# Folding layer 3's router weights: queries first, on quarters of TensorE's columns

## The chip, the cores and the metric

The kernel runs on one core of a Trainium2 chip. The metric is the device time of one execution in microseconds (us), given as the median of several runs. A core has five engines with a queue of instructions each: TensorE (PE in the profile; its loads of weights are PEld) multiplies matrices into the accumulation memory, PSUM; VectorE (DVE), ScalarE (ACT) and GpSimd (POOL) work element by element; SyncE (SP) issues most of the DMA transfers. The engines run side by side and wait for each other through semaphores.

## The reference

The input has 8 blocks of 128 tokens with 512 numbers each. Four layers follow one another, each a "conditioned" part and a feed-forward part whose result is added to x. Only layer 3's last part matters here. Its conditioned part gives y = base(x) + 2 * (low-rank experts), and its feed-forward part picks 16 of 64 experts by the scores

```python
q = jnp.einsum('bsd,rd->bsr', x, Wq_w)          # Wq_w: 16 x 512
scores = jnp.einsum('bsr,er->bse', q, keys)     # keys: 64 x 16
top_vals, top_idx = jax.lax.top_k(scores, TOP_K)
```

where this x is y, so `base = jnp.einsum('btd,od->bto', x, W)` (W: 512 x 512) and the experts' output matrix B (512 x 128 in all) come before it. Scores are linear in y, so the kernel never forms y: it folds keys, Wq and W into one matrix of 512 x 64 (the "fk" product), which is applied to x, and keys, Wq and B into one of 128 x 64 (the "gk" product), which is applied to the gated middle of the experts. Products of three matrices can be taken in two orders: (keys Wq) first, then times W; or (Wq W) first, then times keys.

## The kernel before

The program is one `forward` of some 2300 lines. A tile framework orders each engine's instructions and sets the semaphores. After layers 0 and 1 comes layer 2's attention, a hand-ordered loop of 32 steps, then the `ending`, which holds layer 2's feed-forward part and layer 3.

`open3` allocates layer 3's tiles in a pool (`w3`) and loads them by SyncE, one transfer after the other: Bm in four transfers, `base` (1 MB), `wq` (each of the four chunks of 128 rows has 16 columns), `keysT` (16 partitions by 64), `wB`, `wmr` (the middle's and the router's weights, with 64 columns left free for the folded scores), and `BwT` (1 MB). SyncE's queue is in order, so a transfer that waits holds up those behind it. The load of the attention's sums for their check (`all`, line 750) follows.

`layer2` multiplies the eight blocks of tokens by layer 2's matrix: `product`, tile `h`, 16 matmuls of 128x128 for each block (line 1753 is the helper's). The matmuls leave their sums in PSUM banks, where `delta` adds the low-rank part for four blocks at a time; then VectorE adds the bank to x (line 1929), which frees it. Between the products, layer 3's weights are prepared by two generators, stepped once a block: `weights_turned` transposes base, wB and wq by TensorE, and `fold_scores` makes the folded score matrices. Their banks have the tag "st" once delta(0) is through, three buffers, which were those of h for blocks 0, 1 and 2. ScalarE copies each result to memory (`copied`, line 1955).

Layer 2's routing runs beside: VectorE, with exponentials on ScalarE at lines 1874 and 1885 (tiles p and m), ends in p, which TensorE transposes (`pT`, line 1901) and turns into `pmix`; VectorE then makes `zp` (line 1910), which delta(0) reads.

`fold_scores` in the kernel before takes keys times the transposed queries (kwp, four matmuls whose contraction has 16 rows), then for each of four chunks of columns four accumulating matmuls with W (fkp, 16 matmuls with 64 columns moved), then four with wBT (gkp).

`layer3` follows: `mids` (midp, tile wmr read), `route` on VectorE, `fold_ranks` (fp, with sums W3s made by GpSimd at line 2003), `mix`, `fold_last` (gp), `scores` (sc), `ranks` (z), `turned` (zT) and `last` (o), which writes the output. GpSimd also makes the sums Bws from BwT[...].

A matmul of 32-bit numbers leaves two records in the profile. If its weights have 32 columns, and its result lies in one of four groups of 32 partitions, it takes a quarter of TensorE's columns. The helper `slot(j)` names such a group, and `mmq` is the matmul without a check of groups; `low` (tile z, 128 columns moved) and the down-projection's low rank (tile td, 256 columns moved, line 362) use quarters already.

Of the kernel before, what the change touches and what calls it, by code (L numbers as in the profile page):

```python
# [10 lines left out]
F32 = mybir.dt.float32  # L11
# [6 lines left out]
P = 128  # L18
NB = 8
NT = NB * P  # L20
D = 512
DC = D // P
# [1710 lines left out]
def ending(  # L1733
    tc, a, out, x, ident, bias3, experts, early, tile_of_w2, tile_of_aw, room, chunks, mm, kept=lambda i: i
# [5 lines left out]
    pe, act, dve, pool, sp = nc.tensor, nc.scalar, nc.vector, nc.gpsimd, nc.sync  # L1740
    NE, NR = 64, 8
# [7 lines left out]
    def slot(j):  # L1749
        return slice(j * 32, (j + 1) * 32)  # L1750

    def mmq(o, lhsT, rhs, start, stop):
        return pe.matmul(o, lhsT, rhs, start=start, stop=stop, skip_group_check=True)  # L1753
# [7 lines left out]
    L3 = SimpleNamespace()  # L1761
# [37 lines left out]
    def turn(y2, b, bank):  # L1799
        if not Y2T:  # L1800
            Y2T.append(early.tile([P, DC, NT], F32, tag="yT", name="y2T"))
        ps = bank("mm", [P, DC, P], f"y2T_{b}")
        for c in range(DC):
            pe.transpose(ps[:, c, :], y2[:, b, c * P : (c + 1) * P], ident)
        (act.copy if b % 2 else dve.tensor_copy)(Y2T[0][:, :, b * P : (b + 1) * P], ps)

    def low(g, bank):

        ps = bank("mm", [P, P], f"z2_{g}")
        for c in range(DC):  # L1810
            for j in range(HB):
                b = g * HB + j
                mmq(ps[slot(j), :], A2[:, c, :], Y2T[0][:, c, b * P : (b + 1) * P], c == 0, c == DC - 1)
        dve.tensor_copy(zq[:, g, :], ps)

    def anchors(g, bank):
        ps = bank("mm", [P, 2, 16], f"hd_{g}")
        for i in range(2):
            t0 = (2 * g + i) * 2 * P
            for c in range(DC):  # L1820
                mm(ps[:, i, :], Y2T[0][:, c, t0 + 1 : t0 + 2 * P : 2], WH[:, c, :], c == 0, c == DC - 1)
        dve.tensor_tensor(
            hd[:, 2 * g : 2 * g + 2, :], ps, b16.unsqueeze(1).to_broadcast([P, 2, 16]), ALU.add
        )
# [8 lines left out]
    def product(b, tag, bank):  # L1833

        ps = bank(tag, [P, DC, P], f"h_{b}")
        for o in range(DC):
            for c in range(DC):
                mmq(
                    ps[:, o, :], W["2"][:, c, o * P : (o + 1) * P], Y2T[0][:, c, b * P : (b + 1) * P],
                    o == 0 and c == 0, False,  # L1840
                )
        H[b] = ps
# [53 lines left out]
    def gains(bank):  # L1896

        p = Z["p"]
        pt = bank("mm", [P, NA, P], "pT2")
        for i in range(NA):  # L1900
            pe.transpose(pt[:8, i, :], p[:, i, :], ident)
        pT = L3.w3.tile([8, NA * P], F32, tag="pT", name="pTs2")
        act.copy(pT, pt[:8].rearrange("p i t -> p (i t)"))
        pm = bank("mm", [P, TG, 64], "pmix")
        for g in range(TG):
            for j in range(HB):
                b = g * HB + j
                mmq(pm[slot(j), g, :], Li, pT[:, b * 64 : (b + 1) * 64], g == 0, True)
        zp = L3.w3.tile([P, TG, P], F32, tag="zp", name="zp")
        dve.scalar_tensor_tensor(  # L1910
            zp.rearrange("p g (t two) -> p g t two", two=2),
            zq.rearrange("p g (t two) -> p g t two", two=2),
            0.5,
            pm.unsqueeze(3).to_broadcast([P, TG, 64, 2]),
            ALU.mult,
            ALU.mult,
        )
        Z["zp"] = zp

    def delta(g):  # L1920

        zp, Bm = Z["zp"], L3.Bm
        for o in range(DC):
            for j in range(HB):
                mmq(H[g * HB + j][:, o, :], Bm[slot(j), o * P : (o + 1) * P], zp[slot(j), g, :], False, True)
        for j in range(HB):
            b = g * HB + j
            t = x[:, :, b * P : (b + 1) * P]
            dve.tensor_tensor(t, H[b], t, ALU.add)
# [3 lines left out]
    def open3(w3, ex_sm):  # L1933
        def load(name, shape, src):
            t = w3.tile(shape, F32, tag=name, name=name)
            sp.dma_start(t, src)
            return t

        L3.w3 = w3
        L3.Bm = w3.tile([P, D], F32, tag="Bm", name="Bm2")  # L1940
        for j in range(4):
            sp.dma_start(L3.Bm[slot(j), :], a["Bmat"])
        L3.base = load("base3", [P, DC, D], chunks(a["base3"]))
        L3.wq = load("Wq3", [P, DC, 16], chunks(a["Wq3"]))
        L3.keysT = load("keysT", [16, NE], a["keysT"])
        L3.wB = load("wB3", [P, D], a["wB3"])
        L3.wmr = w3.tile([P, DC, WR], F32, tag="wmr3", name="wmr3")
        sp.dma_start(L3.wmr[:, :, 0:136], chunks(a["wmr3"]))
        L3.Bw = load("BwT", [P, DC, D], chunks(a["BwT"]))
        L3.steps = experts("l3", L3.wmr, "logits", 2.0, bias3, None, None, x, None, width=WR)  # L1950
        L3.zgT = w3.tile([P, DC, NT], F32, tag="zgT", name="zgT")

    def copied(shape, name, ps, dst=None):
        t = L3.w3.tile(shape, F32, tag=name, name=name) if dst is None else dst
        act.copy(t, ps)
        return t

    def weights_turned(bank):

        L3.W = L3.w3.tile([P, DC, D], F32, tag="W3", name="W3")  # L1960
        for o in range(DC):
            ps = bank("mm", [P, DC, P], f"W3p_{o}")
            for d in range(DC):
                pe.transpose(ps[:, d, :], L3.base[:, d, o * P : (o + 1) * P], ident)
            copied(None, None, ps.rearrange("p c d -> p (c d)"), L3.W[:, o, :])
            yield
        ps = bank("mm", [P, DC, P], "wB3p")
        for o in range(DC):
            pe.transpose(ps[:, o, :], L3.wB[:, o * P : (o + 1) * P], ident)
        L3.wBT = copied([P, DC, P], "wB3T", ps)  # L1970
        yield
        ps = bank("mm", [P, D], "wq3p")
        for o in range(DC):
            pe.transpose(ps[:16, o * P : (o + 1) * P], L3.wq[:, o, :], ident)
        L3.wqT = copied([16, D], "wq3T", ps[:16])

    def fold_scores(bank):
        ps = bank("mm", [P, DC, NE], "kwp")
        for o in range(DC):
            mm(ps[:, o, :], L3.wqT[:, o * P : (o + 1) * P], L3.keysT, True, True)  # L1980
        kw = copied([P, DC, NE], "kw3", ps)
        yield
        ps = bank("mm", [P, DC, NE], "fkp")
        for d in range(DC):
            for o in range(DC):
                mm(ps[:, d, :], L3.W[:, o, d * P : (d + 1) * P], kw[:, o, :], o == 0, o == DC - 1)
        copied(None, None, ps, L3.wmr[:, :, 136:WR])
        yield
        ps = bank("mm", [P, NE], "gkp")
        for o in range(DC):  # L1990
            mm(ps, L3.wBT[:, o, :], kw[:, o, :], o == 0, o == DC - 1)
        L3.GK = copied([P, NE], "gk3", ps)


# [191 lines left out]
    def layer2(y2, bank, held=lambda: None, do=range(NB)):  # L2186

        for b in do:
            turn(y2, b, bank)
        for g in range(TG):  # L2190
            if g or len(do) > HB:
                low(g, bank)
                anchors(g, bank)

        where = ["mm"]

        def free(tag, shape, name):
            return bank(where[0], shape, name)

        turning, folding = weights_turned(free), fold_scores(free)  # L2200
        for b in range(HB):
            if b not in H:
                product(b, "av" if b == HB - 1 else "st", bank)
                next(turning)
        routing()
        gains(bank)
        product(HB, "av", bank)
        next(turning)
        delta(0)
        where[0] = "st"  # L2210
        for b in range(HB + 1, NB):
            product(b, "mm", bank)
            for _ in turning:
                pass
            next(folding, None)
        delta(1)

    def layer3(bank, between=lambda: None):
# [37 lines left out]
    return SimpleNamespace(  # L2256
        prepare=prepare, load_w2=load_w2, load_aw=load_aw, turn=turn, low=low, anchors=anchors,
        product=product, shifted=shifted, open3=open3, layer2=layer2, layer3=layer3,
    )

# [64 lines left out]
```

## Time and profile before

| | us |
|---|---|
| median of 3 runs | 1501.79 |
| lowest and highest run | 1498.33, 1505.07 |
| the profiled execution | 1500.54 |
| its span, first to last instruction | 1498.7 |
| TensorE busy | 1483.4 |
| VectorE busy | 1066.7 |
| GpSimd busy | 855.7 |
| ScalarE busy | 562.5 |
| granted TensorE clock, share of full speed | 0.997 |

All times in views of the trace are counted from the first instruction of the profiled execution. A line of the timeline has start, length, engine, line of code, operation, result and operands, shape and count; in brackets stands how long the engine was idle before, and what ended the idle time. The chain of waits is followed back from the last instruction: at each step to what released it, or to the instruction before it on its engine. The prefix "in_" marks an input in device memory; buffer numbers are left out of names.

### The profile page before, as it was taken

How to read it: one execution, taken by the hardware profiler on the slowest of the kernel's cores; microseconds unless marked ns; L12 is line 12 of the kernel's file. 1: busy time of each engine (PE TensorE's matmuls, PEld its weight loads, DVE VectorE, ACT ScalarE, POOL GpSimd, SP SyncE). 2: the span in 40 equal slices, each digit the busy share in tenths (PEclk: the TensorE clock that was granted, in tenths of full speed). 3: DMA queues.
4: the chain of work that ended last, by engine and by line, in shares of the span. 5: the costliest groups of instructions: out<-in, count | busy, mean ns of one | idle time of the engine just before them, and what ended most of it. 6: DMA issues, size and time to landing. Idle time of an engine off the chain costs nothing.

```text
span 1498.7 us, 18133 instructions
## 1 busy us (share of the span) xinstructions
PE 1483.4 (99%) x5629; PEld 943.6 (63%) x5629; DVE 1066.7 (71%) x2121; ACT 562.5 (38%) x1422; POOL 855.7 (57%) x874
## 2 busy tenths in 40 slices
PE   9999999999999999999999999999999999999998
PEld 7888787455555655555555555565555565559887
DVE  4566524388888787877778778787878878854475
ACT  1111101044444554454554444455444455431110
POOL 2232103567776777777777777677777777621210
PEclk9999999999999999999999999999999999999999
DMA  7311001313646444554454455345445534432001
GB/s 240 118 43 33 1 1 51 97 32 102 172 136 206 139 120 130 154 183 127 134 150 127 125 150 179 121 134 159 126 129 164 167 106 138 120 106 93 2 6 54
DMA packets 154985, 171.43 MB, mean 114 GB/s; under 512 B 52480, under 2 KB 125376, under 8 KB 154752
## 3 DMA queue, kind: packets, MB, share of 16 engines
q1 hardware_dynamic: 136736, 133.17, 30.2%
q0 software_dynamic: 17056, 36.49, 7.9%
q8 instruction: 47, 0.77, 0.2%
q10 hardware_dynamic: 1088, 0.52, 0.1%
q14 instruction: 58, 0.48, 0.1%
HBM read 129.35 MB, written 40.76 MB: 114 GB/s over the span
## 4 chain that ended last, share of the span: by engine, by line
PE 91%; DVE 4%; DMA 2%; POOL 1%; issue 1%; ACT 0%; SPq 0%; ACTq 0%; DVEq 0%; POOLq 0%
PE st L1165 17%; PE av L1217 17%; PE g L362 8%; PE q_six L971 8%; PE wo_two L971 6%; PE q_one L971 5%; PE q_five L971 5%; PE dn L362 5%; PE wo_six L971 4%; PE wo_one L971 4%; PE eo_l L53 3%; PE h L1753 2%; PE z L1753 2%; PE midp_l L53 1%; PE o L1753 1%
## 5 line engine op out<-in xcount | busy, mean ns | idle before, releaser
L914 POOL DMA_INDIRECT kn<-in_k_cache,kvrow_k x256 | 270.3, 1056 | 77.1 <-issue 70.9
L914 POOL DMA_INDIRECT vals<-in_v_cache,kvrow_v x256 | 271.6, 1061 | 73.5 <-issue 58.4
L1217 PE MATMUL av<-pT,vals 128*128 128x512 f32 x640 | 290.7, 592 | 0.2 <-DVE oT L1227 0.2
L1169 ACT ACTIVATE pT<-st,hide 128x512 f32<-128x512 f32 x256 | 176.0, 687 | 194.0 <-PE st L1165 173.1
L1165 PE MATMUL st<-qT,kT 128*128 128x512 f32 x512 | 237.7, 597 | 1.0 <-DMA qT<-turned_new 0.8
L1217 PEld LDWEIGHTS av<-pT,vals 128*128 128x128 f32 x640 | 121.4, 190 | 152.7 <-issue 149.0
L1070 POOL TENSOR_TENSOR vq<-q,txq 128x256 f32<-128x256 f32 x128 | 121.2, 978 | 135.1 <-ACT sqq L1044 95.6
L1165 PEld LDWEIGHTS st<-qT,kT 128*128 128x128 f32 x512 | 96.9, 191 | 111.7 <-issue 104.8
L1185 DVE TENSOR_TENSOR part<-pT 128x512 f32<-128x512 f32 x128 | 88.4, 692 | 76.9 <-ACT pT L1169 66.7
L971 PE MATMUL q_one<-q,x 128*128 128x384 f32 x256 | 93.0, 486 | 0.0
L1044 ACT ACTIVATE sqq<-q 128x128 f32<-128x128 f32 x252 | 78.2, 310 | 11.8 <-DVE q L1020 5.1
L971 PEld LDWEIGHTS q_one<-q,x 128*128 128x128 f32 x256 | 48.5, 190 | 39.8 <-issue 14.1
L971 PE MATMUL q_six<-q_s,xs_all 128*128 128x384 f32 x192 | 69.8, 486 | 0.0
L1025 ACT COPY q<-q_one 128x256 f32<-128x256 f32 x32 | 11.9, 372 | 150.4 <-PE q_one L971 133.5
L971 PE MATMUL wo_one<-o,oT 128*128 128x256 f32 x256 | 65.8, 379 | 0.2 <-DVE oT L1227 0.2
L1165 PE MATMUL st<-qT,kTn 128*128 128x512 f32 x128 | 65.4, 592 | 0.0
L971 PE MATMUL wo_two<-o_s,os 128*128 128x256 f32 x256 | 60.6, 380 | 1.8 <-DVE vals L1020 1.5
L429 POOL TENSOR_TENSOR ws<-wu 128x256 f32<-128x256 f32 (+1 forms) x9 | 6.4, 713 | 91.8 <-DMA wu<-in_WuT 81.0
L1169 ACT ACTIVATE pT<-st,rs 128x512 f32<-128x512 f32 x64 | 44.0, 687 | 38.5 <-PE av L1217 25.7
L971 PEld LDWEIGHTS wo_one<-o,oT 128*128 128x128 f32 x256 | 48.6, 190 | 13.8 <-issue 0.5
L1201 ACT COPY rows<-rows 32x32 f32<-32x32 f32 x96 | 20.7, 216 | 92.8 <-DVE rows L1196 64.2
L362 PE MATMUL g<-xs,ws 128*128 128x256 f32 (+1 forms) x240 | 55.2, 379 | 0.0
(459 smaller groups left out, 2853.0 us busy)
## 6 DMA issues: line engine op xcount, KB each, us to landing
turned_new<-qkt SPq DMA_DIRECT2D x120, 160.0 KB
turned_cached<-kt SPq DMA_DIRECT2D x128, 128.0 KB
kT<-turned_cached SPq DMA_DIRECT2D x32, 512.0 KB
R<-sums SPq DMA_DIRECT2D x32, 512.0 KB
qT<-turned_new SPq DMA_DIRECT2D x30, 512.0 KB
q<-in_WqT SPq DMA_DIRECT2D x8, 1024.0 KB
o<-in_WoT SPq DMA_DIRECT2D x8, 1024.0 KB
kn<-in_k_cache,kvrow_k POOLq DMA_INDIRECT x256
```

Of the source, the lines that this page charges most:

```text
L53: pe.matmul(o, lhsT, rhs, start=start, stop=stop)
L362: pe.matmul(o, lhsT, rhs, start=start, stop=stop, skip_group_check=True)
L914: kept(pool.indirect_dma_start(out=d[:, c, :], out_offset=None, in_=kc if what == "k" else vc, in_offset=bass.IndirectOffsetOnAxis(ap=kvro ...
L971: kept(pe.matmul(o, l[:, c, :], r[:, c, :], start=start and c == 0, stop=c == 1, skip_group_check=True))
L1044: kept(act.activation(sq, S[n][m][:, j, i, :], AF.Square, accum_out=S[n]["ssq"][:, j, col : col + 1]))
L1070: kept(pool.tensor_tensor(to, t[:, b, :, hi : hi + 64], wx[:, b, lo : lo + 64].unsqueeze(2).to_broadcast(list(to.shape)), ALU.mult,))
L1165: kept(pe.matmul(ps, s["kT"][:, c, 4 * j : 4 * j + 4, :] if c < 4 else s["kn"][:, j], s["qT"][:, :, REP * j : REP * (j + 1), :].rearrange( ...
L1169: kept(act.activation(pT[:, c, :, :].rearrange("p i t -> p (i t)"), ps, AF.Exp, **(dict(bias=hide[:, b, c : c + 1]) if c < 4 else dict(bia ...
L1185: kept(dve.tensor_tensor(o, l, r, ALU.add))
L1201: kept(act.copy(rows[0:32, g, :], rows[32 * g : 32 * g + 32, 0, :]))
L1217: kept(pe.matmul(ps, v[:, c, :], pT[:, c, :, :].rearrange("p i t -> p (i t)"), start=c == 0, stop=c == NC - 1, skip_group_check=True,))
L1753: return pe.matmul(o, lhsT, rhs, start=start, stop=stop, skip_group_check=True)
```

## The change

The query weights get a tile of 32 columns a chunk, of which 16 are loaded, and the keys a tile of 128 partitions: both are set to zero by GpSimd, and the keys are then loaded four times, to partitions 0, 32, 64 and 96. The transposition of wq falls away. `fold_scores` takes the queries first: for each chunk o of 128 rows it multiplies the queries' chunk by W's chunk in quarter o of the columns. The four quarters hold four partial sums on four groups of partitions. The product with the repeated keys then contracts over all 128 partitions and so adds the quarters; the rows between are zero. The same is done with wBT. `weights_turned` has one step less, so the calls of `next` are given a default.

```diff
         L3.base = load("base3", [P, DC, D], chunks(a["base3"]))
-        L3.wq = load("Wq3", [P, DC, 16], chunks(a["Wq3"]))
-        L3.keysT = load("keysT", [16, NE], a["keysT"])
+        L3.wq = w3.tile([P, DC, 32], F32, tag="Wq3", name="Wq3")
+        L3.keys = w3.tile([P, NE], F32, tag="keys4", name="keys4")
+        for t in (L3.wq, L3.keys):
+            pool.memset(t, 0.0)
+        sp.dma_start(L3.wq[:, :, 0:16], chunks(a["Wq3"]))
+        for j in range(4):
+            sp.dma_start(L3.keys[32 * j : 32 * j + 16, :], a["keysT"])
         L3.wB = load("wB3", [P, D], a["wB3"])
...
         L3.wBT = copied([P, DC, P], "wB3T", ps)
-        yield
-        ps = bank("mm", [P, D], "wq3p")
+
+    def fold_scores(bank):
+        ps = bank("mm", [P, D], "qwp")
         for o in range(DC):
-            pe.transpose(ps[:16, o * P : (o + 1) * P], L3.wq[:, o, :], ident)
-        L3.wqT = copied([16, D], "wq3T", ps[:16])
-
-    def fold_scores(bank):
-        ps = bank("mm", [P, DC, NE], "kwp")
+            mmq(ps[slot(o), :], L3.wq[:, o, :], L3.W[:, o, :], True, True)
+        qw = copied([P, D], "qw3", ps)
+        ps = bank("mm", [P, P], "qbp")
         for o in range(DC):
-            mm(ps[:, o, :], L3.wqT[:, o * P : (o + 1) * P], L3.keysT, True, True)
-        kw = copied([P, DC, NE], "kw3", ps)
+            mmq(ps[slot(o), :], L3.wq[:, o, :], L3.wBT[:, o, :], True, True)
+        qb = copied([P, P], "qb3", ps)
         yield
         ps = bank("mm", [P, DC, NE], "fkp")
         for d in range(DC):
-            for o in range(DC):
-                mm(ps[:, d, :], L3.W[:, o, d * P : (d + 1) * P], kw[:, o, :], o == 0, o == DC - 1)
+            mm(ps[:, d, :], qw[:, d * P : (d + 1) * P], L3.keys, True, True)
         copied(None, None, ps, L3.wmr[:, :, 136:WR])
-        yield
         ps = bank("mm", [P, NE], "gkp")
-        for o in range(DC):
-            mm(ps, L3.wBT[:, o, :], kw[:, o, :], o == 0, o == DC - 1)
+        mm(ps, qb, L3.keys, True, True)
         L3.GK = copied([P, NE], "gk3", ps)
...
-                next(turning)
+                next(turning, None)
         routing()
         gains(bank)
         product(HB, "av", bank)
-        next(turning)
+        next(turning, None)
```

## The prediction

> **What bounds the kernel now.** I read the busy line of the page first, then the chain of waits over the stretch that the change touches, then the timelines of ScalarE, VectorE, GpSimd and SyncE there, to see what stands beside the chain.
>
> ```profile
> PE 1483.4 (99%) x5629; PEld 943.6 (63%) x5629; DVE 1066.7 (71%) x2121; ACT 562.5 (38%) x1422; POOL 855.7 (57%) x874
> ```
>
> TensorE is busy for 99% of the span, so the question is whether its instructions in this stretch are themselves the chain. The chain of waits from 1374 to 1404 us (start, length, engine, tile, line, records; an fp32 matmul leaves two records, a transpose one):
>
> ```profile
> 1380.71 4.87 PE h L1753 x64
> 1385.58 0.44 PE wB3p L1969 x4
> 1386.02 0.44 PE wq3p L1974 x4
> 1386.45 0.89 PE h L1753 x8
> 1387.34 1.03 PE kwp L53 x8
> 1388.37 2.88 PE h L1753 x24
> 1391.25 3.52 PE fkp L53 x32
> 1394.77 3.63 PE h L1753 x32
> 1398.40 0.84 PE gkp L53 x8
> 1399.24 1.10 PE h L1753 x32
> ```
>
> Every piece is TensorE and each begins where the last ends: nothing is waited for. So each microsecond of TensorE taken out here is a microsecond of the chain, until another engine is late. Per record, fkp (64 columns moved) takes 3.52/32 = 0.110 us, no less than h (128 columns), 3.63/32 = 0.113. And h after kwp takes 2.88 for 24, where 24 x 0.112 = 2.69 would do: going back from a 16-row matmul to full ones costs 0.19.
>
> How fast are quarters of the columns? The chain at the down-projection shows the same form, 128 rows by 32 columns, 256 moved:
>
> ```profile
> 171.91 4.89 PE td L362 x88
> ```
>
> That is 0.056 us a record, where full matmuls of 256 take 0.215 (wo_six, 0.86 for 4). The four quarters run side by side: 3.9 times. For the switch into and out of quarters, and the price of 512 moved columns, the chain near the place itself:
>
> ```profile
> 1358.97 1.12 PE h L1753 x10
> ...
> 1360.88 0.34 PE z L1753 x4
> 1361.22 0.42 PE h L1753 x2
> ...
> 1419.31 3.44 PE gp L53 x8
> ```
>
> z x4 is two matmuls on two quarters, so two steps in time of 0.11: 0.34 has 0.12 for entering. The two h records behind it take 0.42 instead of 0.22: 0.20 for leaving. gp gives 0.43 for each record of 512.
>
> **What the Trainium skill says.** "TensorE: Matmul & The Clock Gate", section "Measured speedup vs the span model", gives 2.38 times for three column tiles at 512 columns; td here reaches 3.9 with four in a long run. "TensorEngine Tiling (Array Packing)", section "Key Properties", says that changing the tiling mode drains the engine; the 0.12 and 0.20 above agree. The first page, section "LDWEIGHTS (loading the stationary operand)", says that loading time goes with the number of weight columns, P/1.2 ns, so 107 ns for 128: fkp's 110 ns a record at 64 moved columns agrees, which is why narrow products are no bargain here. No run shows quarters at 512 columns.
>
> **The change part by part, on TensorE.** Removed: wq3p 0.44, kwp 1.03, the 0.19 of leaving kwp's 16 rows, fkp 3.52, gkp 0.84: together 6.02 us.
>
> Added, the queries on the quarters (qwp, four matmuls of 512 moved columns, eight records): 0.12 for entering, then two steps of 0.43, the four quarters together: 0.98. Bounds: two quarters at a time, four steps, 1.84; one at a time, eight, 3.56. td decides for four at a time, since it too moves a different tile through each quarter. Then qbp, eight records of 128 columns in two steps: 0.22. Leaving to h: 0.20. The new fkp has 4 matmuls with 128 weight columns instead of 16: 8 x 0.11 = 0.88; the new gkp one: 0.22. Together 2.50 us. Gain on TensorE: 6.02 - 2.50 = 3.5 us.
>
> In the built program TensorE's order is otherwise the same: h for block 5, wB3p, qwp, qbp, h for block 6, fkp, gkp, h for block 7, delta. Waits that are new there: qbp needs the copy of wB3T. It ran from 1386.05 to 1386.64, and qwp would hold TensorE from about 1385.94 to 1386.83, so about 0.1 us is spare; qwp is the only cover, and without it TensorE would stop for some 0.7 us. fkp needs qw and qb, copies of some 0.59 and 0.3 us, behind which stand 32 records of h, 3.6 us. Banks: qwp and qbp take those of h for blocks 1 and 2, freed by VectorE by 1384.3.
>
> **Beside it.** ScalarE's copies become 0.59 (as wB3T's, of the same shape) and some 0.3 (between 0.21 for gk's 64 columns and 0.37 for kw's 256) in place of 0.57 and 0.37; ScalarE is idle for microseconds on both sides, so nothing. GpSimd gets two memsets, 128 and 64 columns, with no wait, after its last sum of y:
>
> ```profile
> 1339.79 0.73 POOL L1252 TENSOR_TENSOR y<-uo,y 128x256 f32<-128x256 f32 x1
> ...
> 1396.92 1.41 POOL L2003 TENSOR_TENSOR W3s<-W,W3s 128x256 f32<-128x256 f32 x2
> ```
>
> GpSimd then stood idle for 26.0 us, so even 2 us for a memset costs nothing. No row shows one; I take 0.3 each. SyncE issues keys four times instead of once, three more at 0.50: wB, wmr, BwT and the load of the sums slip by 1.6 us. The semaphores rotate too: BwT now waits for base's landing, and its 1 MB moves after it. Before, all these transfers were done by 1361.2 (the DMA share is 0.87 up to there, 0.01 after). BwT is first read at 1375.46 and wB at 1385.3, so some 10 us are spare.
>
> Two other engines' orders move. VectorE takes zp ahead of the two tests of the sums; these end near 1379.7 instead of 1379.0, before its next work at 1381.83. ScalarE takes the exponential m of layer 2's routing behind the first two copies of W3:
>
> ```profile
> 1369.90 0.23 ACT L1885 ACTIVATE m<-m 128x32 f32<-128x32 f32 x1 [1.32 <-DVE m L1884]
> 1371.80 1.07 ACT L1955 COPY W<-W3p 128x512 f32<-128x512 f32 x2 [1.67 <-PE W3p L1964]
> ```
>
> ```profile
> 1371.63 0.19 DVE L1893 TENSOR_TENSOR p<-p,s 128x32 f32<-128x32 f32 x1
> ```
>
> From m's start to p's end VectorE needs 1371.82 - 1369.90 = 1.92. Now m starts when the copies end, 1372.87, and p is there at 1374.8. TensorE first reads it in pT, at 1375.55 in the timeline: 0.7 us are left, so I cost it at nothing; gone, each further microsecond stops TensorE.
>
> **What is late next.** After the gain the first product with W3s comes at 1403.1 instead of 1406.65, and GpSimd's W3s, not moved, ends at 1398.33: 4.8 us to spare. The later steps of layer 3 alternate TensorE and VectorE on data that all move with the chain, and no load stands in them. So 3.5 us should reach the end.
>
> The profiled execution took 1500.54 us (span 1498.7 and 1.84 around it): 1500.54 - 3.5 = 1497.0. The median is 1.25 us above that execution, so against the median, 1501.79 - 3.5 = 1498.3. I forecast the median.
>
> **Rivals.** (1) The quarters don't run together at 512 columns: two at a time gives a gain of 2.7, 1499.1; one at a time also for qbp leaves 0.3, 1501.5. For it: no row at 512. Against: td. (2) The change is done but the gain is lost later, because layer 3's route or GpSimd's sums take up the slack: 1501.8. For it: VectorE holds part of that chain from 1406 to 1410. Against: these steps start from TensorE's own results. (3) Slower: m behind the copies. Place: ScalarE's queue at L1885, then p, pT, pmix, zp, delta. It starts to cost when p comes later than 1375.55, and outweighs the gain when p is 3.5 later than that, 4.2 beyond my estimate. If the two copies waited for a late W3p, say by 6 us, the stall of 5.3 less 3.5 gives 1503.6. For it: the order is really moved. Against: W3p stands in TensorE's own stream, so it can hardly be late alone.
>
> **How the numbers follow.** Forecast 0.76, rival 1 0.09, rival 2 0.09, rival 3 0.06. What a measurement can tell from no change is about 0.5%, 7.5 us. The forecast is half of that. Times spread from 1498.33 to 1505.07, so a median of three moves by about 2 us, and the level that I start from as well. The forecast's own range, with costs from 2.7 to 4.2 and this spread, is 1494.5 to 1502; rivals 1 and 2 lie in it or just above, so 1494 to 1502.5 leaves under 2 in 10 out. Faster by over 0.5% needs double the gain or a lucky median: 0.15. Slower by over 0.5% is rival 3 at its worst: 0.05. Within: 0.80.
>
> **What would show it.** From the first record of wB3p to the first of the second delta: 13.75 us before, about 10.2 after. qwp's eight records should start in two groups of four, 0.43 apart; eight starts 0.43 apart are rival 1. pT should have no wait on VectorE; one is rival 3. GpSimd's W3s should end before the first product that reads it. And the distance from the second delta to the end should be the same in both; if it grows by the gain, rival 2. I'm wrong if the span falls by less than 2 or more than 5 us.

## The result and the profile after

In the first comparison the changed kernel took 1495.38 us (median of 11 runs, 1491.97 to 1501.8), the kernel before 1501.51 (11 runs, 1494.18 to 1505.07): ratio 0.9969, 95% interval 0.9956 to 0.9982. In a second one, of 22 runs against 57, the ratio was 0.9979 (0.9968 to 0.9989). The forecast of 1498.3 against 1501.79 is 0.9977. The page of the changed kernel:

```profile
PE 1476.2 (99%) x5603; PEld 937.3 (63%) x5603; DVE 1069.6 (72%) x2121; ACT 561.9 (38%) x1422; POOL 855.0 (57%) x876
```

Its chain of waits where the change lies (start, length, engine, tile, line, records):

```profile
1381.20 0.44 PE wB3p L1974 x4
1381.63 1.00 PE qwp L1753 x8
1382.63 0.22 PE qbp L1753 x8
1382.85 3.77 PE h L1753 x32
1386.62 0.84 PE fkp L53 x8
1387.46 0.22 PE gkp L53 x2
1387.68 4.73 PE h L1753 x64
```

TensorE is busy 7.2 us less, and the chain is still TensorE alone. The last line is h of block 7 (32 records) and the second delta (32). From the first record of wB3p to the first of the second delta it is 10.20 us, 13.75 before: 3.55 us saved where the forecast has 3.5. But the span fell by 7.1, from 1498.7 to 1491.6. So there were two questions: where do the other 3.5 us come from, and did the 3.55 reach the end? The records answer the second against the forecast: from the second delta to TensorE's last record it is 93.54 us before and 93.90 after. 0.36 us is given back. (From the start of that record to the end of the span, which holds the output's last transfer, it is 5.95 us in one and 6.44 in the other, and between 6.05 and 8.11 in the other profiles.) A fall of the span by more than 5 us was also one of the prediction's own signs of being wrong; the first experiment takes that up.

The timeline shows a change beside the chain as well. ScalarE, then VectorE, then GpSimd in the changed kernel, each with start, length, line, operation and in brackets the idle time ahead (odd and all are the tiles of the check of the attention's sums):

```profile
1367.42 1.07 ACT L1960 COPY W<-W3p 128x512 f32<-128x512 f32 x2 [3.22 <-PE W3p L1969]
1368.38 0.24 ACT L1885 ACTIVATE m<-m 128x32 f32<-128x32 f32 x1
```

```profile
1368.65 0.18 DVE L1886 TENSOR_SCALAR m<-m 128x32 f32<-128x32 f32 x1 [3.16 <-ACT m L1885]
...
1370.12 0.62 DVE L1893 TENSOR_TENSOR p<-p,s 128x32 f32<-128x32 f32 x1
...
1373.42 0.86 DVE L751 TENSOR_SCALAR odd<-all 128x256 f32<-128x256 f32 x1
1374.32 0.70 DVE L752 TENSOR_SCALAR all<-all 128x256 f32<-128x256 f32 x1
```

```profile
1369.97 1.41 POOL L2004 TENSOR_TENSOR W3s<-W 128x256 f32<-128x256 f32 x2 [7.45 <-issue]
1371.35 1.40 POOL L2004 TENSOR_TENSOR Bws<-BwT 128x256 f32<-128x256 f32 x2
```

The same tests and the first sums in the kernel before:

```profile
1371.74 0.28 DVE L751 TENSOR_SCALAR odd<-all 128x256 f32<-128x256 f32 x1
1372.06 0.29 DVE L752 TENSOR_SCALAR all<-all 128x256 f32<-128x256 f32 x1
```

```profile
1374.09 1.41 POOL L2003 TENSOR_TENSOR W3s<-W 128x256 f32<-128x256 f32 x2 [7.18 <-issue]
```

m stands behind two copies, as foreseen, and VectorE waits 3.16 us for it. Not foreseen: the last step of p takes 0.62 us, not 0.19, and the tests odd and all 0.86 and 0.70, not 0.28 and 0.29. In the kernel before, these steps are over when GpSimd's sums begin; in the changed kernel they stand beside them.

### The profile page after: what moved, and what is told of

It reads as the page before. It is cut to its first block, busy times and chain, and to the rows that moved or that the text cites. A ratio compares the mean times of both kernels' runs of the same rounds, so it can differ in the third digit from the quotient of the medians.

```text
span 1491.6 us, 18090 instructions
## 1 busy us (share of the span) xinstructions
PE 1476.2 (99%) x5603; PEld 937.3 (63%) x5603; DVE 1069.6 (72%) x2121; ACT 561.9 (38%) x1422; POOL 855.0 (57%) x876
## 4 chain that ended last, share of the span: by engine, by line
PE 91%; DVE 3%; issue 2%; DMA 2%; ACT 0%; POOL 0%; SPq 0%; ACTq 0%; DVEq 0%; POOLq 0%
PE st L1165 18%; PE av L1217 17%; PE g L362 8%; PE q_six L971 8%; PE q_five L971 6%; PE q_one L971 5%; PE wo_two L971 5%; PE dn L362 5%; PE wo_six L971 4%; PE wo_one L971 4%; PE h L1753 2%; PE z L1753 2%; PE eo_l L53 2%; PE o L1753 1%; PE midp_l L53 1%
```

## The experiments

The table has distances in us between starts of TensorE's records, from one profiled execution of each kernel: the start of wB3p; from the last transpose of y2T (layer 2's input) to pT; from there to the second delta; the stage, from wB3p to the second delta; from the second delta to TensorE's last record. The last column is the ratio of the timed runs, with its interval, where a kernel was timed.

| kernel | wB3p at | y2T to pT | y2T to second delta | stage | delta to end | ratio to before |
|---|---|---|---|---|---|---|
| before | 1385.41 | 14.94 | 38.56 | 13.75 | 93.54 | |
| before, again | 1384.68 | 14.94 | 38.56 | 13.75 | 93.53 | 0.9995 (0.9986 to 1.0005) |
| changed | 1381.03 | 14.94 | 35.01 | 10.20 | 93.90 | 0.9969 (0.9956 to 0.9982) |
| changed, again | 1381.92 | 15.33 | 35.40 | 10.20 | 93.90 | 0.9979 (0.9968 to 0.9989) |
| one quarter | 1382.31 | 15.05 | 38.66 | 13.74 | 93.90 | 0.9999 (0.9985 to 1.0013) |
| two quarters | 1385.05 | 14.97 | 36.43 | 11.60 | 93.90 | |
| split fold | 1377.51 | 14.94 | 35.29 | 10.48 | 93.90 | |
| late m | 1381.39 | 18.15 | 36.66 | 10.20 | 93.91 | |
| sums of Bw later | 1383.56 | 14.94 | 35.01 | 10.20 | 93.91 | |
| before with memsets | 1382.17 | 15.33 | 38.95 | 13.75 | 93.91 | |
| memsets on VectorE | 1385.31 | 14.42 | 34.49 | 10.20 | 93.41 | 0.9976 (0.9968 to 0.9984) |
| other layout | | 13.86 | 32.83 | | 94.01 | 0.9966 (0.9952 to 0.9979) |
| both | | 13.11 | 32.30 | | 93.64 | 0.9963 (0.9948 to 0.9978) |

**Both kernels once more, without an edit.**

> The kernel before once more, unchanged. Stage here and in all runs below: from the first record of wB3p to the first record of the second delta. My theory (the change saves 3.55 us in that stage and nothing ahead of it): the stage is 13.75 us, within 0.1, whenever it starts, and the first record of wB3p may lie several us away from the 1385.41 of the first profile, since TensorE's clock in the first 32 us differs from run to run. Rival (the loads or memsets of the change also save some 4 us ahead of the stage): wB3p starts near 1385.4 again, within 1 us. Ratio to the kernel before: 1.000, within 0.002.

> The changed kernel once more. My theory: stage 10.2 us, within 0.1; the start of wB3p is free to move by several us; the ratio to the kernel before is 1 - 3.5/1500 = 0.9977, within 0.0015. Rival (4 us more are saved ahead of the stage): wB3p starts near 1381.0 again, within 1 us, and the ratio is near 0.995.

The stages repeat to 0.01 us, the distance to the end as well. The start of wB3p doesn't: over the kernels it lies anywhere from 1377.51 to 1385.41, with no order by what is changed (before with memsets 1382.17, memsets on VectorE 1385.31). The second profile of before came 0.7 us earlier than its first, that of changed 0.9 later than its first, so by the word of the expectation this pair alone leaves the rival standing; the other kernels of the table, and the ratio of 0.9979 over 22 runs, speak against it. So does where the gap opens. Counted record by record, TensorE starts layer 0's tile dn (at 165.3 us in the first profile of before) 3.5 us earlier in changed, but 4.5 earlier in before again, the same program; at wB3p the two are 4.4 and 0.7 ahead. Much of the 4.4 us can be put down to the granted clock. Two stretches ahead of the place, first in before, then in changed (stretch, its length, busy time and records of PE, PEld, DVE, ACT and POOL, granted clock, DMA share, GB/s):

```profile
24.00:32.00 8.00, 6.11 (x33) 4.39 (x32) 4.76 (x27) 1.58 (x5) 0.11 (x1) 0.79 0.79 219
1300.00:1340.00 40.00, 39.40 (x155) 23.22 (x154) 24.31 (x45) 14.83 (x26) 13.67 (x15) 0.96 0.39 113
```

```profile
24.00:32.00 8.00, 7.72 (x47) 6.24 (x46) 4.08 (x17) 1.85 (x6) 0.00 (x0) 1.00 0.67 211
1300.00:1340.00 40.00, 39.36 (x152) 21.91 (x151) 25.37 (x45) 13.06 (x23) 13.00 (x14) 1.00 0.38 113
```

Before lacks 0.21 of the clock over 8 us and 0.04 over 40: as an estimate, 1.7 + 1.6 = 3.3 us of TensorE's time that changed doesn't lose. In the second pair the second stretch has 0.91 in before and 0.96 in changed, so it differs between executions of one program. The timed runs agree: a straight line through the 22 runs of changed and the 57 of before gives 1.3 us less for each 0.001 of mean granted clock, and at equal clock changed is 2.9 us faster (95% interval 2.0 to 3.8). So nothing ties the 4.4 us to the change, and the span, on which the prediction set its sign of being wrong, was a poor measure: it fell by 7.1 us in the first pair and by 3.9 in the second.

The second profile of changed has a line among TensorE's waits (who waited for what, total, times, longest) that the first lacks:

```profile
PE pT L1901 <- DVE p L1893: 0.2, 1, 0.2
```

pT came 0.39 us later after y2T, and the second delta with it. So the routing does run out of slack in some executions.

**Queries first, without the side by side of the quarters.** The results of all four chunks add up in one quarter, and the keys contract 32 rows:

```diff
-            mmq(ps[slot(o), :], L3.wq[:, o, :], L3.W[:, o, :], True, True)
-        qw = copied([P, D], "qw3", ps)
+            mm(ps[slot(0), :], L3.wq[:, o, :], L3.W[:, o, :], o == 0, o == DC - 1)
+        qw = copied([32, D], "qw3", ps[slot(0)])
```

(the same for qbp; fkp and gkp then read `L3.keys[slot(0)]`). For two quarters, `slot(o % 2)` and 64 rows.

> Queries first, but without the four quarters: the four matmuls of qwp add up in one quarter of 32 columns, those of qbp too, and the keys contract 32 rows. My theory (the gain comes from the quarters running side by side): qwp is eight steps of 0.43 = 3.4 us in place of two, qbp eight of 0.11 = 0.9 in place of two; the stage is 10.2 + 2.5 + 0.7 = 13.4 us, and the time is that of before within 0.1%. Rival (taking the queries first is what saves, because 64-column products are gone, and the quarters add little): the stage stays below 11 us.

> The changed kernel with qwp and qbp on two quarters of the columns, each adding two of the four matmuls, and the keys on 64 rows. My theory (as many run together as there are quarters in use): qwp takes four steps of 0.43 = 1.72 in place of 0.86, qbp 0.44 in place of 0.22; stage 10.2 + 0.86 + 0.22 = 11.3 us. Rival (matmuls that add up in one quarter don't overlap with the neighbour's): as on one quarter, 13.4.

The chain with one quarter, and then with two:

```profile
1382.91 3.55 PE qwp L53 x8
1386.46 0.87 PE qbp L53 x8
1387.33 3.77 PE h L1753 x32
1391.10 1.03 PE fkp L53 x8
```

```profile
1385.65 1.84 PE qwp L1753 x8
1387.49 0.44 PE qbp L1753 x8
1387.93 3.77 PE h L1753 x32
1391.70 1.03 PE fkp L53 x8
```

Eight steps of 0.43, four, two: qwp takes 3.55, 1.84 and 1.00 us, with 0.12 of entering in each. The stages exceed the expectations by 0.3 us, 0.19 of it in fkp: I had counted no price for going over to a contraction of 32 or 64 rows, and it takes 1.03 in place of 0.84; the other 0.14 stands in the piece of h behind gkp (64 records in 4.87, in place of 4.73). With one quarter nothing is left of the gain (13.74 against 13.75, ratio 0.9999): taking the queries first in this form is worth nothing without the quarters. Of the 3.54 us between one quarter and four, 2.55 lie in qwp and 0.65 in qbp, the quarters side by side, and 0.33 in the contraction over fewer rows. Other ways to take the queries first, with W as the weights and 16 columns moved, were not run.

**The switch into and out of quarters.** One more `yield` ahead of qbp:

```diff
         qw = copied([P, D], "qw3", ps)
+        yield
         ps = bank("mm", [P, P], "qbp")
```

> The changed kernel with one more stop: qbp stands behind h of block 6 and fkp and gkp behind h of block 7, so TensorE enters and leaves the quarters twice. My theory (0.12 to enter, 0.20 to leave): stage 10.2 + 0.32 = 10.5 us, and the h behind qwp shows 0.2 more than 32 x 0.112. Rival (the switch has no price of its own): 10.2.

```profile
1378.11 1.00 PE qwp L1753 x8
1379.11 3.77 PE h L1753 x32
1382.88 0.36 PE qbp L1753 x8
1383.23 3.77 PE h L1753 x32
```

The stage is 10.48, 0.28 more. Both h take 3.77 where 32 x 0.112 = 3.58: 0.19 for leaving, each time; qbp takes 0.36 where it was 0.22: 0.14 for entering. The price exists and is near what was read from the profile of before.

**How much the routing can be late.** Twelve copies of m onto itself on ScalarE:

```diff
+        for _ in range(12):
+            act.copy(m, m)
         act.activation(m, m, AF.Exp, scale=-2.0)
```

> The changed kernel with twelve copies of m onto itself on ScalarE ahead of its exponential: 12 x 0.24 = 2.9 us more on the way to p. The scheduler answers by putting seven matmuls of h (1.55 us) ahead of pT. My theory (slack of 0.4 us at pT in the changed kernel's trace): TensorE waits 2.9 - 0.4 - 1.55 = 0.9 us at pT, and the distance from the last y2T transpose to the second delta grows by that. Rival (the routing has several us of slack, because TensorE does other work first): no wait at pT and no growth.

TensorE waits at pT for VectorE's p, 1.5 us, and the second delta comes 1.65 us later after y2T. The expectation of 0.9 was too small by 0.75, and the parts are: m starts 3.01 later, not 2.9; from m's start to p's end VectorE takes 2.84 us where it took 2.36 in the first profile of changed; and 0.15 us lie between p's end and pT's record wherever pT waits. So a delay of m goes to TensorE in full once the slack is gone, and rival 3's mechanism is real; only its size was small.

**Why VectorE is slow there.** A copy of 16 columns on GpSimd that waits for W3's last part holds back the sums of Bw:

```diff
+        pool.tensor_copy(
+            tw.rearrange("p k s i c -> p (k s i) c")[:, :, 0:1],
+            L3.W[:, 3, 0:16].unsqueeze(2),
+        )
         S["b"] = [left_sums(*left(L3.Bw, k), tw[:, k], pool) for k in range(2)]
```

> The changed kernel with a small copy on GpSimd (16 columns of W3's last part into Bws, overwritten afterwards) ahead of its sums W3s and Bws, so that these start after 1377 us, when VectorE's p and the tests of the sums are over. My theory (VectorE's longer times there come from GpSimd's sums beside them): p 0.62 becomes 0.19, odd 0.86 becomes 0.28, all 0.70 becomes 0.29; TensorE's stage stays 10.2 us. Rival (the times belong to the place in VectorE's order, whatever GpSimd does): 0.62, 0.86 and 0.70 again.

VectorE's timeline in this kernel:

```profile
1372.23 0.44 DVE L1891 TENSOR_SCALAR s<-s 128x4 f32<-128x4 f32 x1
1372.71 0.18 DVE L1892 RECIPROCAL s<-s 128x4 f32<-128x4 f32 x1
1372.92 0.46 DVE L1893 TENSOR_TENSOR p<-p,s 128x32 f32<-128x32 f32 x1
...
1375.95 0.29 DVE L751 TENSOR_SCALAR odd<-all 128x256 f32<-128x256 f32 x1
1376.27 0.29 DVE L752 TENSOR_SCALAR all<-all 128x256 f32<-128x256 f32 x1
```

odd and all are back at 0.29. p is not: the first two sums W3s had stayed ahead of the small copy and ran from 1371.92 to 1373.3, over L1891 (0.44, else 0.17) and L1893 (0.46, else 0.19). The edit missed its aim for p, but what it did speaks for the cause: of the same VectorE program only instructions that GpSimd's sums stand beside are long. Over all thirteen profiles it is so: the step at L1893 takes 0.19 us in the five without a sum beside it and 0.46 to 0.62 in the other eight, odd 0.28 to 0.29 in four and 0.32 to 0.86 in nine. The Trainium skill says so in "SBUF — State Buffer", section "Who interferes with whom": VectorE and GpSimd share a pair of ports, and tensor_scalar in its two-port modes and tensor_tensor with two inputs in SBUF wait for a GpSimd instruction in progress, while tensor_reduce doesn't. The runs agree: L753, a tensor_tensor, takes 0.83 beside the sums in changed and 0.43 here, the tensor_reduce at L755 0.42 in both.

**The memsets alone.** Two memsets of the same size in the kernel before, into tiles that nothing reads:

```diff
+        for k, n in ((0, 128), (1, NE)):
+            pool.memset(w3.tile([P, n], F32, tag=f"pad{k}", name=f"pad{k}"), 0.0)
         L3.wq = load("Wq3", [P, DC, 16], chunks(a["Wq3"]))
```

> The kernel before with the two memsets on GpSimd alone (128 and 64 columns, into tiles that nothing reads), nothing else of the change. In the built program they move m on ScalarE behind the first two copies of W3, as the change did. My theory (the 0.36 us that every changed kernel gives back 48 us after the second delta comes from GpSimd's program, which the memsets shift: its second sums xs start at 43.02 in place of 43.32 us after the second delta, and beside them VectorE's zg takes 0.80 in place of 0.42): 43.02, 0.80, and 93.90 us from the second delta to TensorE's last record; from m's start to p's end 2.3 to 3.0 us in place of 1.92; stage 13.75. Rival (the new fold itself shifts the sums): 43.32, 0.42 and 93.54, as in the kernel before.

My theory's numbers came: 93.91 to the end; 3.03 us from m's start to p's end, at the top of what was expected; stage 13.75. Not in the expectation, pT comes 0.39 later. First GpSimd's sums in before and in this kernel, then VectorE's line that is hit, in before and in this kernel:

```profile
1442.48 1.41 POOL L2003 TENSOR_TENSOR xs<-x 128x256 f32<-128x256 f32 x2 [18.11 <-issue]
```

```profile
1438.94 1.41 POOL L2005 TENSOR_TENSOR xs<-x 128x256 f32<-128x256 f32 x2 [17.83 <-issue]
```

```profile
1445.14 0.42 DVE L2145 TENSOR_TENSOR zg<-zg,gate 128x256 f32<-128x256 f32 x1
```

```profile
1441.89 0.80 DVE L2147 TENSOR_TENSOR zg<-zg,gate 128x256 f32<-128x256 f32 x1
```

GpSimd waits for a record of z before it overwrites its old sums. In the four profiles of the table without such memsets on GpSimd it starts 0.81 us after that record's start, in the nine with them 0.52. Its sums then stand 0.3 us earlier. zg's product with the gate starts 45.97 us after the second delta in both; in the kernel before a new sum starts just behind it (46.06) and it is the sum that is long (0.93), with the memsets the sum starts ahead of it (45.75) and zg takes 0.80 us instead of 0.42. The last four records of that group of transposes zT, which wait for zg, start 0.37 late. Why two memsets a hundred us earlier shorten this reaction by 0.3 us stays open. One lead stands in the traces: a packet on DMA queue q14, which the page marks "instruction", starts 0.64 us after the late start of the sums in just those four profiles, and in the nine it is not there but some 23 us earlier (19.5 to 19.7 us after the second delta), ahead of GpSimd's wait. Whether it has to do with the delay no run tests.

**The memsets on VectorE.**

```diff
         for t in (L3.wq, L3.keys):
-            pool.memset(t, 0.0)
+            dve.memset(t, 0.0)
```

> The changed kernel with the two memsets on VectorE in place of GpSimd. In the built program m stands ahead of the copies of W3 on ScalarE again. My theory: the second sums xs start 43.32 us after the second delta, zg takes 0.42 there, 93.54 us from the second delta to TensorE's last record; 1.92 from m to p and no wait at pT; stage 10.2; so the whole 3.55 us reaches the end, ratio to the kernel before 0.9976. Rival (the 0.36 belongs to the new fold): 43.02, 0.80 and 93.90.

zg is at 0.42 again, m ahead of the copies, p ready 3.72 us ahead of pT. The two memsets take 0.17 and 0.11 us. The ratio is as expected; the parts are better than that: y2T to delta fell by 4.07 and not by 3.55, since the scheduler now takes the products z and hd of layer 2 in one go each:

```profile
1361.64 0.64 PE h L1753 x4
1362.28 1.00 PE z L1753 x28
1363.28 1.99 PE hd L53 x16
```

That is 3.63 us, where h, z, hd, h, z, hd took 0.42 + 0.34 + 1.04 + 0.32 + 0.99 + 1.05 = 4.16 before. Another 0.13 us goes at fp. So this run differs from changed by more than the 0.36 and the routing. It has a side effect that cost nothing here: VectorE reaches the memsets only at 1360.68, SyncE's queue stands from base to 1360.87 for the query weights behind them, and the loads that follow start 9 to 11 us later after base than in changed. From y2T to the last record: 132.10 before, 128.91 and 129.30 in the two profiles of changed, 127.90 here.

**Another layout.** The chain shows 20 transposes without any wait (W3p, wB3p). They turn back what the host's layout has turned, so W3 and wB3T can be loaded as they are used:

```diff
-        L3.base = load("base3", [P, DC, D], chunks(a["base3"]))
+        L3.W = load("W3", [P, DC, D], chunks(a["base3"]))
...
-        L3.wB = load("wB3", [P, D], a["wB3"])
+        L3.wBT = load("wB3T", [P, DC, P], chunks(a["wB3"]))
...
-    h["base3"] = i["L3_cond_W"].T
+    h["base3"] = i["L3_cond_W"]
```

(wB3 likewise; `weights_turned` becomes empty.)

> The changed kernel with base and wB handed over in the other layout, so that W3 and wB3T are loaded as they are used and the 20 transposes (four W3p groups, wB3p) with their five copies on ScalarE are gone. My theory (TensorE is the chain from the last turn of y to the second delta without a gap): 20 x 0.11 = 2.2 us less from the last y2T transpose to the second delta, and some 2.2 us less in all (ratio to the changed kernel 0.9985). m no longer stands behind copies, so p comes some 2.8 us earlier and pT, 1.3 us earlier on TensorE, finds it there. Rival (the transposes only filled time in which TensorE would have waited for the routing): pT waits for VectorE and less than 1 us is saved.

> Both together: base and wB in the other layout, without the 20 transposes, and the memsets on VectorE. My theory: 32.8 us from the last y2T transpose to the second delta (2.2 less than changed), 93.54 from there to TensorE's last record, no wait at pT; 5.7 us less than before, ratio 0.9962. Rival (the 0.36 us stays, since GpSimd's sums are shifted by W3's earlier arrival as well): 93.9 to 94.0, ratio 0.9964.

2.18 us less from y2T to the second delta, with pT 1.08 earlier and no wait: the transposes were work on the path, not filling. On the same chip the median was 1495.54 against 1497.91 for changed. With the memsets on VectorE as well, the distance to the end is 93.64, 0.10 above the expectation, and it is 125.94 us from y2T to the last record, 6.16 less than before, and 1491.65 us in all against 1497.45 for the kernel before: the fastest version tried, by the trace 3.0 us ahead of the changed kernel. The intervals of their ratios overlap, so the order of these two rests on the trace.

## Why the prediction was right, and where not

- **TensorE's sum** was right: 6.02 removed, 2.50 added, 3.5 gained; measured 3.55. Its terms: qwp 0.98 (measured 1.00), qbp 0.22 (0.22), leaving 0.20 (0.19), fkp 0.88 (0.84), gkp 0.22 (0.22). Taking td's four at a time for 512 columns held: the eight records start at 1381.56 to 1381.58 and 1382.02 to 1382.04, two groups 0.45 apart. Rival 1 falls. Its 2.7 for two at a time was too high: two quarters gained 2.15, since qbp takes two steps more as well (0.22) and the contraction over fewer rows costs 0.33. And fkp's 0.110 us a record, which the prediction sets beside a load time, is a spacing: each weight load of fkp itself lasts 0.192 us in the trace.
- **Covers.** qbp's wait for wB3T was covered: the copy ended at 1382.25, the first qbp record starts at 1382.45 (0.1 forecast as spare, 0.2 found). fkp found its inputs behind h. GpSimd's W3s ended at 1394.65, first read at 1398.72: 4.1 us spare, 4.8 forecast. The loads on SyncE cost nothing: GpSimd's Bws, which reads BwT, followed W3s at 1371.35 without a wait.
- **"GpSimd gets two memsets ... costs nothing"** is the step that failed, a small one beside a sum that held. Their own 0.20 and 0.15 us do hide (0.3 each forecast), but alone they cost the kernel before 0.37 us at zT and 0.39 at pT, by its trace. I asked what hides them, and not what their presence reorders on other engines.
- **"0.7 us are left" for p** was mis-sized. The term is "VectorE needs 1.92": beside GpSimd's sums it needs 2.34 to 3.03 in the five profiles that leave the routing as changed has it (changed twice, one quarter, two quarters, split fold). From p's end to pT's start it is 0.45 at best, and in three of the five pT was late, by 0.03 to 0.39.
- **"From the second delta to the end the same"**: 0.36 longer. Rival 2 had GpSimd's sums among its places, as takers of slack; a tenth of the gain did go to them, but through VectorE's zg, which they slow. Rival 3's mechanism showed with 0.39 at the most, never near the 3.5 that it needed.
- **The whole.** By the traces 2.8 to 3.2 us of the 3.55 reach TensorE's last record, 0.9979 to 0.9981 of the time. The forecast's 0.9977 was a little high in gain, and both measured intervals hold it. The median of 1495.38 lay 2.9 below the forecast of 1498.3; the second comparison, with more runs, has 0.9979, so this was the spread of the executions, which is larger than what the change is worth. That the first median came out so low is luck.

## What to carry to other kernels

Where TensorE is the chain, small weight tiles (32 columns) on its four quarters ran 3.9 times as fast as on one here, and the sum over the quarters came free with a next contraction over all 128 rows; a visit cost about 0.3 us, so visit once. Even an operation that costs nothing by itself is an input to the scheduler and to the engines' timing: compare the order of every engine, and for each step that moves ask what it now stands beside, since VectorE and GpSimd slowed each other here. Where the effect is 0.2% of a time that spreads over 0.7%, measure distances between records inside the trace: the stage and the distance to the end repeated to 0.01 us.

## What the runs showed of the hardware

- At 512 columns moved, a 32-bit product on one, two and four quarters took 3.55, 1.84 and 1.00 us. Without 0.12 for entering it is 3.43, 1.72 and 0.88: 3.9 times for four. Records of one quarter that add up overlap with the neighbour's just as independent ones do.
- Contracting 32 or 64 rows in place of 128 costs a switch too: 0.19 us more in fkp, 0.14 behind gkp.
- A VectorE instruction of 0.19 us took up to 0.78 beside GpSimd's sums of 0.72 each; where VectorE started first, the sum took 0.93.
- Over 79 runs of two kernels, 0.001 less of mean granted clock went with 1.3 us more of 1500.
- GpSimd's reaction to the same record was 0.81 or 0.52 us, to 0.01 us in all profiles of the one kind and of the other, decided by two memsets on GpSimd a hundred us ahead; the cause is open.
